# Two silus at a time in the loop, roundings by ScalarE behind it, and the last scales ahead of the comparison

## The chip, the core and the metric

The kernel runs on one core of a Trainium2 chip. The metric is the device time of one execution in microseconds (us). A core has TensorE (PE in the profile: matmuls and transpositions), VectorE (DVE), ScalarE (ACT), GpSimd (POOL), and SyncE (SP), which issues transfers. Each engine takes its own list of instructions in order; semaphores make it wait for the others.

## The reference

One transformer layer on x of 2048 tokens with 256 features, and a context of 1601 tokens of 256 features:

```
# cross attention: latents are the layer-normalised x, keys are context and latents
q = LN(latents) @ W_q;  k, v = concat(LN(ctx) @ W_kv, LN(latents) @ W_kv)
sim  = rms(q) * scale @ rms(k).T           # 4 heads of 64, masked context keys at -max
x    = x + softmax(sim) @ v @ W_out + b_out
# feed-forward on y = layernorm(x), hidden size 1024
aq(t) = clip(round(t * s), -128, 127) / s, s = 127 / max|t| per token
wq(w) = ternary weights over their mean magnitude
h = aq(y) @ wq(w1).T
h = depthwise convolution over tokens, three taps and a bias, for each hidden channel
h = silu(h)
out = x + aq(h) @ wq(w2).T
```

Rounding to integers is done by adding a large constant (MAGIC, 12582912) and taking it off again: in f32 the addition leaves an integer.

## The kernel before

`layer` is written twice: once with a cheap bound for the softmax shift (`behind` is a tile that receives a flag), and a second time, exact, behind a branch that runs only if the flag counts a row for which the bound was too far off. In the runs shown the second copy is not entered. All instructions are issued through a helper (`InOrder`, line 170) that keeps them in the written order on each engine, so nearly all rows of the profile say L170 and are told apart by their tiles.

**Prologue.** Normalised tokens are projected to q, k and v, and the two weights w1 and w2 are made ternary.

**Loop.** There are eight units (four groups of 512 queries, two pairs of heads each) of ten beats; a beat takes three blocks of 128 keys, the last beat of a unit two. In a beat TensorE makes the scores of the next beat (`st<-q_un,kT`), ScalarE takes their exponentials (`pt<-st`), and TensorE multiplies the present beat's exponentials with v (`ot<-pt,v_sb`). `pt` has six buffers; the score banks ("big") have three, and are shared with the feed-forward. The rows of exponentials are summed partly by VectorE (`vec`), partly by adding transfers (`acc`, `acd`) that POOL issues.

The feed-forward is laid beside the attention by a plan: `at(k, call, when)` notes a call for beat k. It works in groups g of 256 tokens (0 to 7), each of four slots (two chunks of 128 hidden channels a slot). A slot's calls in `feed_forward` (982) are `hidden` (matmuls to `ph`), `dequantize` (VectorE, `h`), `taps` and `last_tap` (ScalarE's `side`, VectorE's and POOL's `pre`), and `silu` (858), which writes `t`. A slot follows two beats (`pace`) after the one before it; its silu stands three beats after its taps. `t` is kept as token by channel with four channels side by side, so a silu writes one f32 every 16 bytes. When a group's slots are done, `magnitudes`, `columns` and `scales` find each token's largest value, `scales_spread` brings the scales back to rows (`tb`), `rounding` (945) multiplies `t` by them and writes the integers to `hq`, and `product` and `output` finish (`py`, `res`). The silu and the exponential stand in different tables of ScalarE, so the program holds a table load (ACT_TABLE_LOAD) wherever the one follows the other. Groups 0 to 3 and the first slot of group 4 have their silus inside the loop.

**Tail.** Behind the loop, `tick(i)` (1150) takes the remaining 15 slots one after another, `head(i)` (1119) first finishes the last four blocks of 128 tokens of the attention (`block_steps`: divide, output projection `po`, residual, normalise `y`, `quantize` (760) to `yq`, and a transposition), and what the plan still holds (group 3's spreading, roundings and products) is taken one call a tick. A tick's order is: silu of the slots two and one ticks ago, `dequantize` of this slot (`h`), outputs that are due, last tap of the slot before, this slot's `pre` and `side` on ScalarE, a group's scales or roundings where they are due, then the `hidden` matmuls of the next slot and the convolution of this one. `ph` has two buffers, so the next `hidden` waits until the silu of the slot before has read its own. A group's two roundings stand in two successive ticks, and its two products behind the second.

At the end group 7 is rounded in four quarters, and `flag` (1134) compares the last unit's denominators, reduces the result over all units, and sums it over the partitions by a matmul (`many`), whose count is copied to `behind`. It comes ahead of `scales_spread` of group 7 there.

Of the kernel before, what the change touches and what calls it, by code (L numbers as in the profile page):

```python
# [10 lines left out]
F32 = mybir.dt.float32  # L11
# [8 lines left out]
P = 128  # L20
# [9 lines left out]
def layer(  # L30
# [62 lines left out]
    ones16 = const.tile([P, P], BF16, name="ones16")  # L93
    nc.vector.memset(ones16, 1.0)

    neg_half = const.tile([P, 2 * H], F32, name="neg_half")
    nc.gpsimd.memset(neg_half, -0.5)

# [530 lines left out]
    with att:  # L629
# [86 lines left out]
                        start=(n == 0), stop=(n == len(terms) - 1),  # L716
                    )

        def compare(u, r):

            if behind is None:
                return
            within = wk.tile([P, QW], BF16, tag="within", name="within")
            vector.tensor_scalar(within, r, math.exp(LAG), None, ALU.is_le)
            vector.scalar_tensor_tensor(within, r, math.exp(-LAG), within, ALU.is_ge, ALU.mult)
            vector.tensor_reduce(near[:, u : u + 1], within, AX.X, ALU.min)


        def block_steps(qb, oT, sub, po):
            box = {}  # L730

            def project_out():
                box["po"] = po()
                for c in range(ND):
                    tensor.matmul(
                        box["po"], oT[:, c, ts(sub, P)], wo_sb[:, c, :],
                        start=(c == 0), stop=(c == ND - 1),
                    )

            def residual():  # L740
                vector.tensor_tensor(x1[qb], box["po"], x1[qb], ALU.add)
                st = sm.tile([P, 6], F32, tag="st3", name="st3")
                box["mv"] = sm.tile([P, 2], F32, tag="mv3", name="mv3")
                vector.bn_stats(st, x1[qb])
                vector.bn_aggr(box["mv"], st)

            def inverse_deviation():
                inverse_root(box["mv"][:, 1:2], LN_EPS, ALU.add, P, (1,), gpsimd)

            def normalize():  # L750
                box["y"] = wk.tile([P, D], F32, tag="y", name="y")
                vector.tensor_scalar(
                    box["y"], x1[qb], box["mv"][:, 0:1], box["mv"][:, 1:2], ALU.subtract, ALU.mult
                )
                vector.tensor_reduce(
                    units1[:, qb : qb + 1], box["y"], AX.X, ALU.max, apply_absolute_value=True
                )
                box["sc"] = quant_scales(units1[:, qb : qb + 1], 1, vector)

            def quantize():  # L760
                vector.tensor_scalar(box["y"], box["y"], box["sc"][:, 0:1], None, ALU.mult)
                box["yq"] = wk.tile([P, D], BF16, tag="yq", name="yq", bufs=2)
                vector.tensor_scalar(box["yq"], box["y"], MAGIC, -MAGIC, ALU.add, ALU.add)

            def transpose():

                t0 = OFF + qb * P
                tp = bank("tpy", [P, 2, P])
                yT = tp[:, 0, :].bitcast(BF16).rearrange("p (c t) -> p c t", c=ND)
                for c in range(ND):  # L770
                    tensor.transpose(yT[:, c, :], box["yq"][:, ts(c, P)], ident16)
                tensor.transpose(tp[:, 1, :], box["cm"][:, 0, :], ident)
                scalar.copy(xq_all[:, :, t0 : t0 + P], yT)
                scalar.copy(ib_all[:, 1 + qb * P : 1 + (qb + 1) * P], tp[:, 1, :])

            def bias():
                gpsimd.tensor_tensor(x1[qb], x1[qb], bo_sb, ALU.add)

            def unit_row():
                product_units(units1[:, qb : qb + 1], 0)  # L780
                box["cm"] = as_rows(units1[:, qb : qb + 1], 1)

            return (
                bias, project_out, residual, inverse_deviation, normalize, quantize, unit_row,
                transpose,
            )
# [158 lines left out]
        def rounding(g, i, tokens=slice(0, G)):  # L945
            b = groups_[g]
            t = b["t"][i][:, tokens, :]
            vector.tensor_tensor(
                t, t, b["tb"][:, tokens].unsqueeze(2).to_broadcast(list(t.shape)), ALU.mult
            )  # L950
            if "hq" not in b:
                b["hq"] = fp.tile([P, G, NH], BF16, tag="hq", name="hq", bufs=1)
            vector.tensor_scalar(
                b["hq"][:, tokens, ts(i, NC2)], t, MAGIC, -MAGIC, ALU.add, ALU.add
            )

        def product(g, i):
            b = groups_[g]
            py = b["py", i] = where["py"]()
            for c in range(NH):  # L960
                tensor.matmul(
                    py, b["hq"][:, ts(i, P), c], w2T[:, c, :], start=(c == 0), stop=(c == NH - 1)
                )
# [18 lines left out]
        def feed_forward(g, k, slots, pace=2):  # L982

            for n in range(slots):
                s, t = g * NP + n, k + n * pace
                for m, call in (
                    (-1, hidden), (-1, dequantize), (0, taps), (1, last_tap), (3, silu),
                ):
                    at(t + m, lambda call=call, s=s: call(s), LATE)
                if n % 2:  # L990
                    at(t + 4, lambda n=n: magnitudes(g, n // 2), LATE)
            if slots < NP:
                return
            t = k + NP * pace
            for m, call in (
                (3, columns), (3, scales), (5, scales_spread), (5, lambda g: rounding(g, 0)),
                (6, lambda g: rounding(g, 1)), (7, lambda g: end_product(g, 0)),
                (7, lambda g: end_product(g, 1)),
            ):
                at(t + m, lambda call=call: call(g), LATE)  # L1000
# [130 lines left out]
                if i < NSUB:  # L1131
                    run(i, RESIDUAL, INVERSE)

        def flag():

            compare(len(units) - 1, r)
            if behind is None:
                return
            worst = sm.tile([P, 1], F32, tag="worst", name="worst")
            vector.tensor_reduce(worst, near, AX.X, ALU.min)  # L1140
            vector.tensor_scalar(worst, worst, 0.5, None, ALU.is_lt)
            many = y_bank("many")[:, :1]
            tensor.matmul(many, ones, worst, start=True, stop=True)
            vector.tensor_copy(behind, many)

        rest = [call for key in sorted(plan) for call in plan.pop(key)]
        slots = list(range(4 * NP + 1, NG * NP))
        N = len(slots)

        def tick(i):  # L1150

            at_ = {i - ((g - 4) * NP - 1) + (g == NG - 1): g for g in range(4, NG)}
            if 0 <= i - 2 < N:
                end_silu(slots[i - 2], 1)
            if 0 <= i - 1 < N:
                end_silu(slots[i - 1], 0)
            if i < N:
                dequantize(slots[i])
            if i >= N and 0 <= i - 1 < N:
                end_last_tap(slots[i - 1])  # L1160
            if 6 in at_:
                magnitudes(at_[6], 1)
                columns(at_[6])
            while outputs:
                output(*outputs.pop(0))
            if 0 <= i - 1 < N and i < N:
                end_last_tap(slots[i - 1])
            if i < N:
                end_taps(slots[i])
            if 6 in at_:  # L1170
                scales(at_[6], at_[6] == NG - 1)
                if at_[6] == NG - 1:
                    flag()
            if 7 in at_ and at_[7] != NG - 1:
                scales_spread(at_[7])
                rounding(at_[7], 0)
            if 8 in at_ and at_[8] != NG - 1:
                rounding(at_[8], 1)
            if 4 in at_:
                magnitudes(at_[4], 0)  # L1180
            if 7 in at_ and at_[7] == NG - 1:
                g = at_[7]
                scales_spread(g, True)
                for n in range(QPG):
                    for half in range(2):
                        rounding(g, half, ts(n, P))
                    product(g, n)
                for n in range(QPG):
                    output(g, n)
            if i + 1 < N:  # L1190
                hidden(slots[i + 1])
            if i < N:
                end_convolve(slots[i])
            if 1 <= i <= NSUB:
                run(i - 1, TURN)
            if 8 in at_ and at_[8] != NG - 1:
                for n in range(QPG):
                    end_product(at_[8], n)
# [54 lines left out]
```

## Time and profile before

| | |
|---|---|
| median of 3 runs (lowest, highest) | 685.49 us (684.77, 688.87) |
| the profiled execution | 688.55 us |
| its span, first to last instruction | 686.7 us |
| busy PE, DVE, ACT, POOL | 629.2, 464.1, 423.8, 276.6 us |
| mean granted TensorE clock | 0.972 |
| the loop's last attend matmul ends | 591.7 us |
| the last output (`res`) on VectorE | 681.89 us |

In the page each digit of a slice is the busy share in tenths of one fortieth of the span; PEclk is the clock that the throttle grants TensorE. A group's row gives the tile written and those read, the shape, the count, then busy us and mean ns, and the idle time before with what ended it. Lines of the order in time give start and length in us.

### The profile page before, as it was taken

What the parts mean: (1) busy time and instruction counts of PE and PEld (TensorE: products, weight loads), DVE (VectorE), ACT (ScalarE), POOL (GpSimd) and SP (SyncE); (2) the same over time, 40 slices, a digit from 0 to 9 for tenths busy, and PEclk for the clock granted to TensorE, in tenths of its full rate; (3) what the DMA queues carried; (4) which work ended last, traced back from release to release, by engine and by line L of the source; (5) the groups of instructions that cost most, each with busy time, mean ns of one, the idle gap of its engine ahead of it and who ended that gap; (6) DMA issues with size and microseconds to landing.
All of it is one profiled execution on the core that took longest, in us unless ns stands there. A gap on an engine that the chain in (4) does not pass through costs nothing. (4 is left out here: it accounts for less than half of the span.)

```text
span 686.7 us, 8000 instructions
## 1 busy us (share of the span) xinstructions
PE 629.2 (92%) x2796; PEld 266.3 (39%) x2796; DVE 464.1 (68%) x770; ACT 423.8 (62%) x535; POOL 276.6 (40%) x331
## 2 busy tenths in 40 slices
PE   4999898999999999999999999998899999857754
PEld 2555563333333333333334333332333333345542
DVE  3658774332832766596378779757966797897885
ACT  1656556554556445669945469998765789545540
POOL 2656673221221234244245433425354446742330
PEclk9999999999999999999999999999999999997975
DMA  7600003685878674478849447693564576100001
GB/s 241 170 0 0 1 1 92 128 161 111 167 140 183 128 148 93 93 154 152 185 96 172 101 107 154 125 182 94 107 123 92 132 138 114 31 0 16 16 16 36
DMA packets 32220, 72.12 MB, mean 105 GB/s; under 512 B 7531, under 2 KB 16940, under 8 KB 32172
## 3 DMA queue, kind: packets, MB, share of 16 engines
q0 software_dynamic: 16560, 60.30, 43.3%
q1 hardware_dynamic: 14524, 10.45, 5.1%
q10 hardware_dynamic: 1088, 0.79, 0.4%
q8 instruction: 24, 0.39, 0.2%
q14 instruction: 24, 0.20, 0.1%
HBM read 9.13 MB, written 2.10 MB: 16 GB/s over the span
## 5 line engine op out<-in xcount | busy, mean ns | idle before, releaser
L170 ACT ACTIVATE pt<-st,bias 128x1024 f32<-128x1024 f32 x232 | 242.8, 1112 | 123.1 <-issue 64.6
L170 PE MATMUL st<-q_un,kT 64*128 64x512 f32 x928 | 223.7, 611 | 4.7 <-DVE res L170 1.8
L170 PE MATMUL ot<-pt,v_sb 128*64 128x512 f32 x928 | 216.6, 600 | 0.0
L170 DVE TENSOR_TENSOR vec<-vec,pt 128x1024 f32<-128x1024 f32 x107 | 136.7, 1278 | 40.2 <-ACT pt L170 36.3
L170 PEld LDWEIGHTS st<-q_un,kT 64*128 64x128 f32 x928 | 83.0, 187 | 124.8 <-issue 91.3
L170 PEld LDWEIGHTS ot<-pt,v_sb 128*64 128x64 f32 x928 | 60.2, 136 | 136.7 <-issue 130.4
L170 POOL DMA_DIRECT2D acd<-pt x54 | 44.9, 831 | 127.9 <-ACT pt L170 61.4
L170 POOL DMA_DIRECT2D acc<-pt x61 | 52.7, 865 | 69.4 <-ACT pt L170 51.7
L170 POOL TENSOR_TENSOR pre<-pre,side 128x512 f32<-128x512 f32 (+1 forms) x32 | 38.3, 1196 | 62.3 <-DVE pre L170 51.4
L170 ACT ACT_TABLE_LOAD x34 | 43.6, 1283 | 16.6 <-DMA lb<-in_L_xattn_ln_l_b_dram 7.4
L170 PE MATMUL kv<-wkv_sb,feat 128*128 128x512 f32 (+1 forms) x116 | 52.9, 599 | 0.0
L170 POOL TENSOR_TENSOR ss<-ss,neg_half 128x8 f32<-128x8 f32 (+1 forms) x23 | 39.1, 1702 | 1.9
L170 ACT ACTIVATE t<-pre 128x512 f32<-128x512 f32 (+1 forms) x32 | 29.7, 928 | 11.8 <-POOL pre L170 11.6
L170 POOL TENSOR_SCALAR cm<-ones,units 128x128 f32<-128x128 f32 x16 | 11.8, 739 | 61.4 <-DVE units L170 57.9
L170 DVE COPY oT<-ot 128x512 f32<-128x512 f32 x8 | 5.5, 691 | 44.6 <-PE ot L170 44.6
L170 DVE TENSOR_REDUCE ss<-sq 128x8 f32<-128x512 f32 (+1 forms) x23 | 15.5, 672 | 29.0 <-ACT sq L170 28.9
L170 DVE TENSOR_TENSOR h<-ph,ib_all 128x516 f32<-128x516 f32 x32 | 21.9, 686 | 19.0 <-PE ph L170 18.6
L170 PE MATMUL ph<-h,dg 128*128 128x256 f32 x90 | 25.8, 428 | 7.4 <-DVE h L170 7.4
L170 DVE RECIPROCAL r<-dn 128x512 f32<-128x512 f32 (+1 forms) x11 | 27.3, 2478 | 5.7 <-PE dn L170 5.7
L170 PEld LDWEIGHTS kv<-wkv_sb,feat 128*128 128x128 f32 (+1 forms) x116 | 21.2, 192 | 21.9 <-issue 20.9
L170 ACT ACTIVATE side<-h,cw_sb 128x256 f32<-128x256 f32 x66 | 29.6, 506 | 0.0
L170 PE MATMUL py<-w2T,hq 128*128 128x256 bf16 x128 | 20.8, 317 | 7.2 <-DVE hq L170 7.2
(129 smaller groups left out, 708.9 us busy)
## 6 DMA issues: line engine op xcount, KB each, us to landing
acc<-pt POOLq DMA_DIRECT2D x61, 512.0 KB, 5.1
acd<-pt POOLq DMA_DIRECT2D x54, 512.0 KB, 4.8
tok<-in_x_dram SPq DMA_DIRECT2D x4, 512.0 KB, 6.1
w_sb<-in_L_ffn_w_dram SPq DMA_DIRECT2D x4, 512.0 KB, 5.3
q_un<-in_x_dram SPq DMA_DIRECT2D x4, 512.0 KB, 3.9
out_dram<-res SPq DMA_DIRECT2D x16, 128.0 KB, 1.7
tok<-in_ctx_dram SPq DMA_DIRECT2D x3, 512.0 KB, 4.7
wkv_sb<-in_L_xattn_W_kv_dram ACTq DMA_DIRECT2D x1, 512.0 KB, 7.2
```

The lines of the kernel that those rows point to most:

```text
L170: return tc.keep_in_program_order(getattr(self.engine, name)(*args, **kwargs))
```

## The change

Three edits, besides a small constant tile `magic` that holds MAGIC and -MAGIC for ScalarE's bias.

1. In the loop the silu of an even slot is put off by one `pace`, to the beat of the following odd slot's silu, so that both run one behind the other.
2. Behind the loop the rounding of `yq` (last four blocks) and of `hq` (groups 3 to 6) is done by two ScalarE instructions each in place of one of VectorE; for `yq` the multiplication by the scale goes along with the first of them. The multiplication of `t` by its scales stays on VectorE, and group 7 keeps its old way.
3. At the end only the two comparisons of the flag stay where they were; the reductions and the sum over partitions come after the first half of group 7's roundings, and the copy to `behind` after its products. The transposition of group 7's scales so comes ahead of the sum.

```diff
-        def compare(u, r):
-
-            if behind is None:
-                return
+        def bounds(r):
             within = wk.tile([P, QW], BF16, tag="within", name="within")
             vector.tensor_scalar(within, r, math.exp(LAG), None, ALU.is_le)
             vector.scalar_tensor_tensor(within, r, math.exp(-LAG), within, ALU.is_ge, ALU.mult)
-            vector.tensor_reduce(near[:, u : u + 1], within, AX.X, ALU.min)
+            return within
...
             def quantize():
+                box["yq"] = wk.tile([P, D], BF16, tag="yq", name="yq", bufs=2)
+                if qb >= NQB - NSUB:
+                    scalar.activation(
+                        box["y"], box["y"], AF.Identity, bias=magic[:, 0:1], scale=box["sc"][:, 0:1]
+                    )
+                    scalar.activation(box["yq"], box["y"], AF.Identity, bias=magic[:, 1:2])
+                    return
                 vector.tensor_scalar(box["y"], box["y"], box["sc"][:, 0:1], None, ALU.mult)
-                box["yq"] = wk.tile([P, D], BF16, tag="yq", name="yq", bufs=2)
                 vector.tensor_scalar(box["yq"], box["y"], MAGIC, -MAGIC, ALU.add, ALU.add)
...
-            vector.tensor_scalar(
-                b["hq"][:, tokens, ts(i, NC2)], t, MAGIC, -MAGIC, ALU.add, ALU.add
-            )
+            hq = b["hq"][:, tokens, ts(i, NC2)]
+            if where["later"] and g < NG - 1:
+                scalar.activation(t, t, AF.Identity, bias=magic[:, 0:1])
+                scalar.activation(hq, t, AF.Identity, bias=magic[:, 1:2])
+            else:
+                vector.tensor_scalar(hq, t, MAGIC, -MAGIC, ALU.add, ALU.add)
...
                 s, t = g * NP + n, k + n * pace
+
+                last = 3 if n % 2 or slots == 1 else 3 + pace
                 for m, call in (
-                    (-1, hidden), (-1, dequantize), (0, taps), (1, last_tap), (3, silu),
+                    (-1, hidden), (-1, dequantize), (0, taps), (1, last_tap), (last, silu),
                 ):
...
-        def flag():
-
-            compare(len(units) - 1, r)
-            if behind is None:
-                return
+        def flag(within):
+
+            u = len(units) - 1
+            vector.tensor_reduce(near[:, u : u + 1], within, AX.X, ALU.min)
             worst = sm.tile([P, 1], F32, tag="worst", name="worst")
             vector.tensor_reduce(worst, near, AX.X, ALU.min)
             vector.tensor_scalar(worst, worst, 0.5, None, ALU.is_lt)
             many = y_bank("many")[:, :1]
             tensor.matmul(many, ones, worst, start=True, stop=True)
-            vector.tensor_copy(behind, many)
+            held["many"] = many
...
                 scales(at_[6], at_[6] == NG - 1)
-                if at_[6] == NG - 1:
-                    flag()
+                if at_[6] == NG - 1 and behind is not None:
+                    held["within"] = bounds(r)
...
                     for half in range(2):
                         rounding(g, half, ts(n, P))
+                    if n == 0 and behind is not None:
+                        flag(held["within"])
                     product(g, n)
+                if behind is not None:
+                    vector.tensor_copy(behind, held["many"])
                 for n in range(QPG):
                     output(g, n)
```

In the list of each engine this takes 16 table loads from ScalarE and adds 24 of its instructions; VectorE loses eight `hq`, four `y` and four `yq` instructions and gains two small constant fills at the start; on TensorE only the `many` matmul changes places with group 7's transposition (`tpb`); the lists of POOL and SP are the same as before.

## Prediction

> **What bounds the kernel now.** I read the slices of the page first, then busy time by stretches, the groups kept apart by shape, and the order in time around the places that change.
>
> ```profile
> PE   4999898999999999999999999998899999857754
> DVE  3658774332832766596378779757966797897885
> ACT  1656556554556445669945469998765789545540
> PEclk9999999999999999999999999999999999997975
> ```
>
> Two regimes: up to slice 34 TensorE is at nine tenths; behind it TensorE falls, VectorE leads and the clock drops in places.
>
> ```profile
> 230.00:592.00 362.00, 354.84 (x1599) 129.19 (x1595) 267.76 (x386) 261.13 (x294) 158.65 (x183) 1.00 0.63 129
> 592.00:630.00 38.00, 25.36 (x117) 16.71 (x117) 31.11 (x74) 14.13 (x31) 14.26 (x24) 0.87 0.01 4
> 630.00:660.00 30.00, 21.74 (x128) 16.83 (x127) 27.18 (x46) 18.31 (x35) 10.54 (x13) 0.99 0.07 23
> 660.00:683.00 23.00, 12.65 (x49) 7.83 (x47) 17.05 (x32) 4.40 (x9) 3.35 (x4) 0.57 0.06 20
> ```
>
> Behind the length stand PE, its loads, DVE, ACT and POOL busy, then clock and DMA. From 230 to 592 TensorE works 354.8 of 362.0 us: the loop is TensorE's. In the tail VectorE works 31.1 of 38 and 27.2 of 30 us: the tail hangs on it and on the chains through it.
>
> **The pairing of the silus.** Each silu in the loop costs ScalarE two table loads, silu's and then exp's again.
>
> ```profile
> L170 ACT ACTIVATE pt<-st,bias 128x1024 f32<-128x1024 f32 x232 | 242.8, 1112 | 123.1 <-issue 64.6 <-PE st L170 43.8 <-DMA acc<-pt 7.7
> L170 ACT ACT_TABLE_LOAD x34 | 43.6, 1283 | 16.6 <-DMA lb<-in_L_xattn_ln_l_b_dram 7.4 <-issue 6.2 <-PE st L170 2.1
> L170 ACT ACTIVATE t<-pre 128x512 f32<-128x512 f32 x17 | 19.5, 1150 | 0.2
> ```
>
> Sixteen slots become eight pairs: 16 loads go, 16 x 1.283 = 20.5 us of ScalarE. The Trainium skill ("ScalarE: Activation LUTs", "Table sets: the hidden batching unit") says to batch activations by table set, and "What ACT_TABLE_LOAD costs" prices a switch at 2.66 us with its drain: 42.6 us by the page, 20.5 by the row, and the trace sides with the row: the load at 584.66 below is followed by its silu at 585.96, with no drain between. On the path either is worth almost nothing, by the waits of 230 to 592:
>
> ```profile
> PE st L170 <- ACT pt L170: 0.8, 2, 0.4
> ```
>
> TensorE waited 0.8 us for an exponential there; gain 0 to 0.8, I take 0. A pair's block is 1.28 + 1.15 + 1.1 + 1.28 = 4.8 us against 3.7 for a single one; a beat takes TensorE 5.5 us and ScalarE 3.1 (three exponentials), so it catches up under the cover of six pt buffers and three score banks. The cover ends with the loop.
>
> ```profile
> 581.53 3.11 ACT L170 ACTIVATE pt<-st,bias 128x1024 f32<-128x1024 f32 x3
> 584.66 1.28 ACT L170 ACT_TABLE_LOAD   x1
> 585.96 1.16 ACT L170 ACTIVATE t<-pre 128x512 f32<-128x512 f32 x1
> 587.13 1.28 ACT L170 ACT_TABLE_LOAD   x1
> 588.42 2.12 ACT L170 ACTIVATE pt<-st,bias 128x1024 f32<-128x1024 f32 x2
> ```
>
> The last pair's block stands before the last two exponentials. It starts at 584.66 as before, since what precedes it waited for a DMA's landing (until 578.3), which isn't touched. They end at 591.6, not 590.5. TensorE's last four attend matmuls (0.95 us, ended 591.7) need the second one, and end at 592.6. All of the tail follows: **+1.0 us** (0 to 1.2).
>
> **The roundings.** Eight hq writes of 128x1024 (g3 to g6) and four y, yq pairs leave VectorE. Each hq takes 0.6 to 1.1 us until the next instruction, 6.9 in sum; y and yq 0.68, so 2.7: relief 9.6 us. ScalarE gets two instructions for each hq, +MAGIC in place and then -MAGIC, the second waiting for the first. The row for 128x1024 is the exponential's, 1.11 us: 2.25 for a pair, 18 us for eight. The y pairs cost 0.60 + 0.49 by the tail's 128x256 pre and side, 4.4 us. Together 22 us.
>
> Is 1.11 right for hq, written in runs of 8 bytes with gaps of 8? The silu of 128x512 takes 1.150 us though half as large; it writes single f32 16 bytes apart. "SBUF — State Buffer" (the note on cachelines under "Door 1") says that SBUF has 16-byte lines and wants two hits in each for full rate. Silu has one, hq four: by the rule 1.11, by the silu row's rate about 2.05. The silu row agrees with the rule; no row shows ScalarE writing four of eight. I take 1.11 and keep 2.05 for the range.
>
> Against the edit speaks "ScalarE: Activation LUTs", "Rules for kernel authors": adds and multiplies belong on VectorE. By that rule alone it loses 22 - 9.6 = 12.4 us. The trace decides by who waits, so I replay the group from h at 645.04 to h at 659.61, 14.57 us.
>
> ```profile
> 647.40 1.22 DVE L170 TENSOR_TENSOR t<-t,tb 128x1024 f32<-128x1024 f32 x1 [1.29 <-ACT tb L170]
> 648.66 0.69 DVE L170 TENSOR_SCALAR hq<-t 128x1024 bf16<-128x1024 f32 x1
> 649.27 0.69 DVE L170 TENSOR_TENSOR h<-ph,ib_all 128x516 f32<-128x516 f32 x1
> 651.52 1.11 DVE L170 TENSOR_SCALAR hq<-t 128x1024 bf16<-128x1024 f32 x1
> 655.67 0.70 DVE L170 TENSOR_TENSOR h<-ph,ib_all 128x516 f32<-128x516 f32 x1
> ```
>
> With the first line's start kept, the multiply lasts until 648.6. VectorE goes on to the next h at 648.65, 0.6 early, and to the second multiply, done by 650.9. ScalarE, in order, rounds from 648.7 to 650.95; only then come its two silus (0.47 apart). The one that frees ph runs 651.35 to 652.05, where it ran 648.67 to 649.40 before, so the next hidden matmuls start at 652.1, not 649.44, and their h at 652.7. ScalarE's pre and side of that tick end near 652.7, the second rounding runs until 655.0, and the product's last 12 matmuls (1.53 us) start at 655.1 instead of 652.69 and end at 656.6. Its outputs (res) stand ahead of the last tap and the following h on VectorE: res until 657.1, tap until 657.5, h from 657.5 instead of 655.67. The remainder, 3.94, is unchanged. So the group takes 16.4 us: +1.85. Two groups show it (g4's and g5's roundings): **+3.7**. Behind g6's no h follows, but the last silu stands behind the second rounding, and the last maximum waits for it: multiply from 662.90 to 664.1, rounding until 666.4, two silus until 667.3, rounding until 669.6, silu until 670.2, maximum from 670.3 instead of 668.83: **+1.5**.
>
> Front (h at 599.76 to h at 630.37, g3's pairs and the four y): until the fifth h VectorE gains 2.7 + 1.8 = 4.5 us. Then h needs hidden, hidden the silu of ph, and that silu stands behind two xq, ib copies (0.5), a rounding (2.25), y and yq (1.1) and another silu (0.5), 4.35 us in all, and the copies wait for a convolution and the transposition of yq behind it (1.53 + 0.1); the lead is lost and 6.0 us stand in the way: -4.5 + 6.0 = **+1.5** (-4.5 to +4).
>
> **The last scales.** Before: from qsc at 672.60 the flag's five VectorE steps, the matmul, the copy, and then the multiply at 676.40. After: the transposition waits for ScalarE's cm alone, so the multiply starts at 674.6, 1.8 earlier. But flag comes after two of the four multiply pairs (1.1 us on VectorE), and its matmul precedes the product's in TensorE's list, which starts near 678.3, not 677.61; its 16 matmuls take 3.8 to 4.2 us at this clock, then paced by TensorE alone. -1.2 to +0.5; **+0.2**. SP and POOL keep their lists, so no DMA changes its place; behind is copied later, yet before the last res.
>
> **Sum.** 1.0 + 3.7 + 1.5 + 1.5 + 0.2 = +7.9 us. The profiled execution took 688.55 us (span 686.7, the rest lies around it) and would take 696.4; it lies 3.06 over the median of the runs. From 685.49 that is **693.4 us**.
>
> **Rivals.** *VectorE's relief arrives, faster.* In the replayed group the delay of the silu and of hidden (2.7 us) meets a cover: hidden ended at 650.0 before, while its h ran only at 653.68, 3.6 us. With VectorE 1.6 us faster (0.6 + 1.0) 2.0 remain. If a rounding held hidden up by less than that, the 9.6 would come through: 9.6 - 1.0 = 8.6 less, 677 us. For it: VectorE is at 27.2 of 30. Against: two dependent 1.11 us. *hq at the silu's rate:* 0.94 x 8 = 7.5 more, 700.9 us; for it the silu row, against it the rule on lines. *A draw:* lead and delay cancel in front and groups, only the loop's end shows: 686.5. *The pairing pays:* 0.8 at most, inside the draw.
>
> **Numbers.** ScalarE's in-order delay, 693.4: 60%, its own range 689 to 699; 14 of these 60 lie within 1%. hq slow: 14%. Relief: 11%. Draw: 15%. About 1% (6.9 us) is what a measurement here tells from no change. Slower by more: 46 + 14 = 60%; within: 14 + 15 = 29%; faster: 11%. The range goes to 683 and 703: TensorE is busy less densely, and the throttle, 0.57 behind 660, may bite more; 677 and a slow hq with such a clock stay outside.
>
> **Right or wrong.** Table loads 18. From 230 to 592 no gain. The last ot near 592.6. In the tail ScalarE over 50 us, with TensorE's hidden waiting for ScalarE's t, h to h per group near 16.4. If the groups take under 14 us, the replay is wrong; if the hq rows show 2 us, its size is.

## The result, and the profile after

The changed kernel takes **697.8 us** (median of 6 runs, 697.15 to 699.57) beside 686.2 for the kernel before on the same chip (6 runs, 684.77 to 688.87): ratio 1.0165, 95% interval 1.0151 to 1.018. It is slower, by 11.6 us in the medians, where 693.4 was forecast. The profiled execution took 697.66 us, its span is 695.9 us against 686.7.

The slices of the page, as shown of before: the loop's part is much the same. In the last six slices VectorE's digits were 8 9 7 8 8 5 and are 7 5 6 6 6 5, and the clock is below nine in the last five slices, where it was in three of the last four.

```profile
PE   4999898999999999999999999998999999647653
...
DVE  3658774333732864795487679568777878756665
ACT  2566556555554555568844468777476589376760
...
PEclk9999999999999999999999999999999999977885
```

The same stretches as before (length, then busy PE, its loads, DVE, ACT and POOL, clock, DMA share, GB/s; the last one is longer by what the kernel is):

```profile
230.00:592.00 362.00, 355.29 (x1601) 129.01 (x1599) 268.36 (x388) 239.82 (x277) 158.39 (x183) 1.00 0.63 129
592.00:630.00 38.00, 22.21 (x101) 15.05 (x98) 24.87 (x57) 19.34 (x40) 13.35 (x22) 0.83 0.00 0
630.00:660.00 30.00, 20.33 (x107) 15.82 (x106) 20.52 (x34) 22.22 (x38) 9.41 (x11) 0.90 0.06 18
660.00:692.00 32.00, 17.12 (x85) 12.39 (x83) 20.56 (x41) 13.19 (x23) 5.20 (x6) 0.76 0.08 27
```

In the loop ScalarE lost 21.3 us of work (261.13 to 239.82) and TensorE's 355 us did not move. In the tail VectorE fell from 31.11 to 24.87 and from 27.18 to 20.52 us, ScalarE rose from 14.13 to 19.34 and from 18.31 to 22.22, and the clock from 630 to 660 went from 0.99 to 0.90. The wait that grew is TensorE's for ScalarE. From 592 on, by the waits (total, times, longest), first before, then after:

```profile
PE ph L170 <- ACT t L170: 5.6, 5, 1.7
```

```profile
PE ph L174 <- ACT t L174: 20.2, 6, 4.9
```

Where the 9.2 us between the two spans lie, by the starts of VectorE's `h` (h0 is the tail's first; h6, h10 and h14 are those of the last slots of groups 5, 6 and 7), the last `qsc` and the last `res`:

| stage | before | after | difference | forecast |
|---|---|---|---|---|
| to the loop's end (first `tpa`) | 591.61 | 590.63 | -0.98 | +1.0 |
| to h0 | 8.15 | 8.15 | 0 | 0 |
| front, h0 to h6 | 30.61 | 34.39 | +3.78 | +1.5 |
| two groups, h6 to h14 | 29.24 | 34.65 | +5.41 | +3.7 |
| behind g6, h14 to last scale | 12.99 | 13.05 | +0.06 | +1.5 |
| last scale to last `res` | 9.29 | 8.53 | -0.76 | together +0.2 |
| last `res` to the end | 4.81 | 6.50 | +1.69 | |
| span | 686.7 | 695.9 | +9.2 | +7.9 |

The median moved by more than the spans since the profiled execution of before lay 2.35 us above its own median and that of after 0.13 below. The spans are read to 0.1 us, and the line of the end with them. The loop's end wanders in the runs below from 589.3 to 593.1 whatever the edit, so that line carries little. The front's +3.78 is loose too. Two runs below, edit 3 alone and the early copy, leave the front as it was, and their fronts take 29.89 and 29.88 us at a clock of 0.89 in place of 30.61 at 0.83, with the same work on VectorE and ScalarE (before, then edit 3 alone):

```profile
599.76:630.37 30.61, 19.64 (x91) 14.27 (x92) 26.71 (x66) 13.51 (x31) 10.11 (x18) 0.83 0.02 5
```

```profile
598.68:628.57 29.89, 19.45 (x90) 14.24 (x91) 26.73 (x66) 13.49 (x31) 10.11 (x18) 0.89 0.02 5
```

A front read from one profile is uncertain by these 0.7 us.

### The profile page after: what moved, and what is told of

Its sections match the earlier page's. It is cut to its first block, busy times and chain, and to the rows that moved or that the text cites. A ratio compares the mean times of both kernels' runs of the same rounds, so it can differ in the third digit from the quotient of the medians.

```text
span 695.9 us, 7999 instructions
## 1 busy us (share of the span) xinstructions
PE 629.7 (90%) x2796; PEld 268.1 (39%) x2796; DVE 455.9 (66%) x756; ACT 420.6 (60%) x543; POOL 276.6 (40%) x331
## 5 line engine op out<-in xcount | busy, mean ns | idle before, releaser
L174 PE MATMUL ph<-xq_all,w1T 128*128 128x258 bf16 x128 | 20.2, 282 | 21.1 <-ACT t L174 20.2
L174 ACT ACTIVATE t<-pre 128x512 f32<-128x512 f32 (+1 forms) x32 | 27.9, 923 | 8.0 <-POOL pre L174 7.9
```

The source lines that it names most:

```text
L174: return tc.keep_in_program_order(getattr(self.engine, name)(*args, **kwargs))
```

## The experiments

Kernels with one edit alone stand on the kernel before; the later ones on these or on the changed kernel. A difference in us is the ratio's excess times 687.2, the median of before in the longer comparisons.

### Edit 1 alone: the pairing

```diff
+                last = 3 if n % 2 or slots == 1 else 3 + pace
...
-                    (-1, hidden), (-1, dequantize), (0, taps), (1, last_tap), (3, silu),
+                    (-1, hidden), (-1, dequantize), (0, taps), (1, last_tap), (last, silu),
```

> The kernel before with the paired silus alone. The prediction's step: loop work of TensorE unchanged, last attend matmul 1.0 us later (592.7), time +1.0 us. The reading of the trace after: a reload of exp waits for the scores that its exponential needs, so with TensorE just behind it the 1.28 us are exposed; eight of these go, one of them at a unit's start near 493 us is worth 1.6 to 1.8 us, and 0.8 us come back at the loop's end: last attend matmul near 590.7, time -1.0 us. Rival (the pairing is what made the kernel slower, by longer ScalarE blocks): +3 us or more.

Ratio 1.0008 (0.9998 to 1.0019, 22 runs): +0.5 us, no difference that it can tell; the 1.0 us less that the reading of the changed kernel's trace had promised did not come. The waits from 560 to 600 of this kernel have a line that the kernels without pairing lack:

```profile
PE ot L170 <- ACT pt L170: 0.8, 1, 0.8
```

Sixteen table loads, 20.5 us of ScalarE, are worth nothing in the loop, and TensorE waits 0.8 us for the last pair at its end.

### The roundings of hq alone, and of y alone

```diff
-            vector.tensor_scalar(
-                b["hq"][:, tokens, ts(i, NC2)], t, MAGIC, -MAGIC, ALU.add, ALU.add
-            )
+            hq = b["hq"][:, tokens, ts(i, NC2)]
+            if where["later"] and g < NG - 1:
+                scalar.activation(t, t, AF.Identity, bias=magic[:, 0:1])
+                scalar.activation(hq, t, AF.Identity, bias=magic[:, 1:2])
+            else:
+                vector.tensor_scalar(hq, t, MAGIC, -MAGIC, ALU.add, ALU.add)
```

> The kernel before with only the hq roundings (groups 3 to 6) on ScalarE; silus single, yq and the flag as before. Theory (ScalarE's order delays the silu that frees ph and the product): h to h over the groups near 16.5 to 17.3 us instead of 14.6, time +7 to +10 us. Rival (VectorE's relief covers it, the loss comes from the flag's place and the clock at the end): -1 to +2 us.

Ratio 1.0087 (1.0069 to 1.0106): **+6.0 us**, a little under the 7 expected. The groups take 17.49 and 17.35 us, as in the changed kernel (17.39 and 17.26): their loss is this edit's alone. The front takes 32.17, +1.56. TensorE's wait for the silu from 592 on (5.6 us before):

```profile
PE ph L174 <- ACT t L174: 15.7, 5, 3.9
```

> The kernel before with only y and yq of the last four blocks on ScalarE. Theory: 0.68 us of VectorE against 1.1 us of ScalarE for each of four, in the stage where VectorE is the tighter of the two: -1 to +1 us. Rival (any rounding on ScalarE is a loss there): +3 us, h to h over the first six slots longer than 30.6 us.

With y and yq alone (the diff of `quantize` above) the ratio is 0.9996 (0.9986 to 1.0006), and the front 29.87, 0.74 less than before. That is the length of the fronts that nothing was changed in (29.89 and 29.88, at the same 0.89), so no gain there is shown to be y's.

### Edit 3 alone: the flag behind the transposition

> The kernel before with only the flag's reductions, sum and copy moved behind half of the last roundings. The prediction: +0.2 us. The reading of the trace after: SyncE reads behind ahead of issuing the last two outputs, and now waits for it; the last res comes 0.5 us earlier or at the same time, the span ends 1 to 2 us later behind it: +1 us. Rival (the earlier transposition pays): -1 us or less.

Ratio 1.0016 (1.0006 to 1.0027): +1.1 us. The last `res` came 8.70 us behind the last scale (before 9.29), yet the end 6.26 us behind that `res` (before 4.81).

The four parts sum to 0.5 + 6.0 - 0.3 + 1.1 = 7.3 us; all together gave 11.3. Of the 4.0 between, 3.0 stand in the front, as far as single profiles tell: 0.8 for the two roundings one at a time, 3.78 with both; counted from a front of 29.9 us it is 2.2. The rest is within the intervals.

### Half the delay: one ScalarE instruction for each hq

```diff
-                scalar.activation(t, t, AF.Identity, bias=magic[:, 0:1])
                 scalar.activation(hq, t, AF.Identity, bias=magic[:, 1:2])
```

This kernel leaves out the addition of MAGIC, so hq is not rounded.

> The kernel with only the hq roundings on ScalarE (groups 3 to 6), each with one instruction instead of two: the addition of MAGIC into t is left out, so hq isn't rounded. Theory (ScalarE's order delays hidden and the product; the prediction put the turning point at a delay of 2.0 us, and half a rounding delays by 2.7 - 1.15 = 1.5): VectorE's relief comes through, h to h per group about 14.4 us or less instead of 17.4, time 2 us under the kernel before, 8 us under the one with both instructions. Rival (the loss comes from handing hq to another engine at all, by an added wait and not by its length): groups above 16 us, +4 us.

Ratio 0.9978 (0.9965 to 0.999), 1.5 us **faster** than before; groups 14.52 and 14.49, clock 1.00. In order of time, one group of it:

```profile
645.47 1.15 ACT L174 ACTIVATE hq<-t,magic 128x1024 bf16<-128x1024 f32 x1 [1.29 <-DVE t L174]
...
646.97 0.68 ACT L174 ACTIVATE t<-ph,cb_sb 128x256 f32<-128x256 f32 x1
...
648.61 0.68 DVE L174 TENSOR_TENSOR h<-ph,ib_all 128x516 f32<-128x516 f32 x1
...
649.43 1.91 PE L174 MATMUL py<-w2T,hq 128*128 128x256 bf16 x16
```

The silu that frees `ph` (`t<-ph`) starts 1.50 us behind the rounding's start, and the next h 3.26 us behind the one at 645.35. One dependent instruction of 1.15 us is hidden; two are not. The groups get no shorter than before all the same: hidden waits 2.27 us for the silu (0.82 before), and VectorE's outputs then wait 1.21 us for the product, which stands behind hidden on TensorE.

### The roundings behind the next silus

```diff
+                pending.append((t, hq))
...
+            late_rounding()
...
-            if 8 in at_ and at_[8] != NG - 1:
+            if 9 in at_ and at_[9] != NG - 1:
                 for n in range(QPG):
-                    end_product(at_[8], n)
+                    end_product(at_[9], n)
```

`late_rounding` issues both instructions of each pending hq; it stands behind the next tick's silus, `pre` and `side`.

> The kernel with only the hq roundings on ScalarE, but each issued behind the next tick's silus, pre and side, and the products of groups 4 to 6 one tick later. The same instructions, 18 us of ScalarE. Theory (their place in ScalarE's list is what costs): hidden no longer waits for them, groups near 14.5 to 16 us, time -1 to +2 us against the kernel before. Rival (the ScalarE work itself is too much for the tail): still +5 us or more.

Ratio 1.0033 (1.0022 to 1.0043): +2.3 us. The later place takes 3.7 of the 6.0 us away. The groups fall to 15.94 and 16.01, not to 14.6: the silu is free, but the products and with them the outputs come a tick later (from the last scale to the last `res` it is 12.67 us, 9.29 before), and the clock stays at 0.89. This run doesn't separate the two.

### Only the first hq on ScalarE, behind the next silus, with y and yq there

```diff
+            if where["later"] and g < NG - 1 and i == 0:
+                pending.append((t, hq))
...
+            late_rounding()
```

> The kernel before with y and yq on ScalarE, and of the hq roundings only the first of each group, issued behind the next tick's silus; the second stays on VectorE. Theory (half of the load fits into ScalarE's gaps and nothing that TensorE needs stands behind it): groups near 14.2 us, time -2 to -3 us against the kernel before, the fastest of all. Rival (any rounding on ScalarE costs): +2 us.

Ratio 0.9963 (0.9946 to 0.998, 14 runs, median 684.89): **2.5 us faster than before**, the best version found. Groups 15.07 and 14.53 (expected near 14.2), front 30.17: neither holds the gain. By the profile it lies behind g6, where h14 to the last scale takes 10.75 us and 12.99 before, with a clock of 0.89 and 0.63; how much of that is the clock's is not separated.

### TensorE kept busy in the changed kernel

```diff
+            if i < N and (i in (2, 3) or 7 in at_ or 8 in at_):
+                for n in range(6 if 8 in at_ else 24):
+                    tensor.matmul(
+                        chunk[slots[i]]["ph"][:, 1, G + 2 : G + 254], w1T[:, 0, 0:P],
+                        xq_all[:, 0, 0:252], start=True, stop=True,
+                    )
```

> The changed kernel with added TensorE matmuls whose result is never read (252 columns, 24 or 6 of them) behind the convolutions of the ticks in which TensorE waits for ScalarE's roundings. They fill idle time only. Theory (the roundings' waits also let TensorE's clock fall, which costs 0.9 us in each group on the product and over 2 us in front): clock 1.0 in the groups instead of 0.90, h to h 16.4 instead of 17.3, and the front 2 us shorter; time -3 to -5 us against the changed kernel, that is +6 to +8 against the kernel before. Rival (the clock doesn't matter, ScalarE alone sets the pace): no change against the changed kernel, +11 us.

Ratio 1.0081 (median 692.86 of 6 runs) in place of 1.0165: 5 to 6 us back from matmuls that nobody reads (the filled-up kernel, below). By stretches (front, two groups, behind g6; the clock stands third from the end):

```profile
601.23:632.68 31.45, 21.71 (x135) 17.61 (x136) 23.30 (x56) 21.34 (x43) 10.12 (x18) 0.95 0.01 5
632.68:649.26 16.58, 13.86 (x100) 11.79 (x99) 11.96 (x21) 12.39 (x22) 5.90 (x7) 1.00 0.08 25
649.26:665.73 16.47, 13.29 (x92) 10.72 (x91) 11.29 (x20) 12.40 (x22) 5.20 (x6) 1.00 0.05 16
665.73:678.48 12.75, 7.70 (x53) 5.70 (x51) 7.90 (x13) 8.03 (x12) 3.75 (x4) 1.00 0.01 3
```

With the clock at 1.00 a group takes 16.58 and 16.47 us, so the excess of the changed kernel's groups over the replay is TensorE's clock. The front takes 31.45 at 0.95, where the changed kernel's took 34.39 at 0.80.

### The copy to behind early

```diff
             tensor.matmul(many, ones, worst, start=True, stop=True)
-            held["many"] = many
+            vector.tensor_copy(behind, many)
```

> The kernel before with edit 3 alone, as in the run of edit 3 alone, but the comparison's result is copied to behind directly after the count `many`, ahead of the two last copies of outputs and not behind the new transposition's work. Theory (GpSimd's closing work, a queue counter 0.86 us and a drain 2.80 us, starts only when behind has been read, and edit 3 made it the last thing to end): from the last res to the end of the span 4.8 us again in place of 6.26, from the last scale to the last res at most 0.6 us more than the 8.70 of edit 3 alone; time about 1 us under that run, 687.0 within 0.7. Rival (the later end has another cause, such as SyncE's load of behind ahead of the last outputs' transfers): last res to end stays near 6.3 and the time near 688.

Ratio 1.0000 (0.9989 to 1.0012) against 1.0016 with the late copy; last scale to last `res` 8.71, last `res` to end 4.83, both as expected; the intervals of the two ratios overlap, so the time alone doesn't settle it. Counted from the last scale the copy comes 1.4 us earlier (5.25 us behind it, 6.61 with the late copy). The theory can be read more sharply in the profiles: in all twelve the end of the span is the later of 8.33 us behind the start of the copy to `behind` and 4.81 us behind the start of the last `res`, within 0.1 us (one within 0.2). The copy is the later in three of them, in bold below, and with the early copy the two are level; a program without GpSimd's drain was not tried.

| kernel | copy + 8.33 | last res + 4.81 | end |
|---|---|---|---|
| before | 684.2 | **686.7** | 686.7 |
| after | **695.9** | 694.2 | 695.9 |
| edit 3 alone | **685.3** | 683.8 | 685.3 |
| early copy | **684.8** | **684.8** | 684.8 |
| filled up | **693.4** | 692.0 | 693.4 |

### The best version with TensorE kept busy

```diff
+                if at_[6] == NG - 1:
+                    keep_warm(24, where["ph"]("warm"))
...
+                keep_warm(6, where["ph"]("warm"))
...
+            if i in (1, 2, 3, 4, N - 1):
+                keep_warm(24 if i == N - 1 else 12, chunk[slots[i]]["ph"])
```

`keep_warm(n, ph)` issues n matmuls like those of the kernel above.

> The run with y on ScalarE and the first hq of each group there behind the next silus (684.89), with matmuls added whose result nobody reads: 12 in the front's four ticks, 24 in the last tick, 24 and 6 behind the last group's two transpositions. If TensorE's clock costs there as the filled-up changed kernel showed (front 2 to 3 us, end about 1 us): granted clock near 1.00 in the front and behind the last group, and 1 to 3 us less, 682 to 684. Rival (the front and the end are set by VectorE's and ScalarE's chain of products and roundings, and the added matmuls stand ahead of needed ones): clock up, time the same or more, 685 to 687.

Ratio 0.9973 (0.9964 to 0.9983, median 685.47), beside 0.9963 without the added matmuls: no gain, the rival's forecast. The mean clock rose from 0.980 to 0.987, but in the profiled execution the front took 32.16 us (30.17 without) and h14 to the last scale 13.29 (10.75). That execution lies 4.7 us above the median of its runs, so these two sizes are not typical; that a higher clock buys nothing here is shown by the times, why it doesn't is not settled.

## Why the prediction was right, and where it was off

The mechanism was the likeliest case's: ScalarE, in order, holds the silu back that frees `ph`, and hidden, h and the outputs follow. Its size was less good: +11.6 us in the medians where +7.9 was forecast. That the two profiles differ by 9.2 is luck in part: front, groups and end lie 4.7 us over their forecasts, the loop's end and the stage behind g6 3.4 under. So is the nearness of the 12.4 us that the sum of busy times gave: the same `hq` instructions at a later place in ScalarE's list cost 2.3 us, not 6.0. Point by point:

**Loop, right.** Table loads are 18, the loop gained nothing, and TensorE waits at its end as worked out:

```profile
584.00 2.13 ACT L174 ACTIVATE t<-pre 128x512 f32<-128x512 f32 x2
...
586.15 1.28 ACT L174 ACT_TABLE_LOAD   x1
...
587.45 2.12 ACT L174 ACTIVATE pt<-st,bias 128x1024 f32<-128x1024 f32 x2
...
588.61 2.08 PE L174 MATMUL ot<-pt,v_sb 128*64 128x512 f32 x8 [0.81 <-ACT pt L174]
...
590.63 0.44 PE L174 MATMUL tpa<-ident,m 128*128 128x128 f32 x2
```

Both silus (584.00), the load, the last two exponentials until 589.57, and the last attend matmuls behind 0.81 us of waiting. Forecast +1.0, shown 0.8 and timed +0.5 (-0.1 to +1.3). Where the loop ended in this profile was luck of the execution: 590.6, not 592.6.

**Size of the rounding, right.** 1.11 us for a run of 128x1024 was taken, 2.05 kept as the rival:

```profile
L174 ACT ACTIVATE hq<-t,magic 128x1024 bf16<-128x1024 f32 x8 | 9.2, 1149 | 0.3
L174 ACT ACTIVATE t<-t,magic 128x1024 f32<-128x1024 f32 x8 | 9.1, 1142 | 4.1 <-DVE t L174 4.1
```

**The groups: steps right, one term missing.** One group of the changed kernel (h at 650.56), to be laid beside the replay:

```profile
654.11 1.15 ACT L174 ACTIVATE t<-t,magic 128x1024 f32<-128x1024 f32 x1 [1.29 <-DVE t L174]
...
655.29 1.15 ACT L174 ACTIVATE hq<-t,magic 128x1024 bf16<-128x1024 f32 x1
...
656.79 0.66 ACT L174 ACTIVATE t<-ph,cb_sb 128x256 f32<-128x256 f32 x1
...
657.51 0.60 PE L174 MATMUL ph<-xq_all,w1T 128*128 128x258 bf16 x4 [3.36 <-ACT t L174]
...
657.95 2.46 PE L174 MATMUL ph<-h,dg 128*128 128x256 f32 x6
...
658.15 0.69 DVE L174 TENSOR_TENSOR h<-ph,ib_all 128x516 f32<-128x516 f32 x1 [0.81 <-PE ph L174]
659.28 1.15 ACT L174 ACTIVATE hq<-t,magic 128x1024 bf16<-128x1024 f32 x1
...
660.20 2.63 PE L174 MATMUL py<-w2T,hq 128*128 128x256 bf16 x16
...
663.88 0.70 DVE L174 TENSOR_TENSOR h<-ph,ib_all 128x516 f32<-128x516 f32 x1
```

Counted from h, the rounding was forecast at 3.7 and stands at 3.55, the silu at 6.3 (6.23), hidden at 7.1 (6.95), its h at 7.7 (7.59), the second rounding's end at 10.0 (9.87). VectorE waits, as foretold, for hidden, and hidden 3.36 us for ScalarE's t. Then the times part: six convolution matmuls take 2.46 us, not 1.46 as in the filled-up kernel, and the product is done at 12.3, not at 11.6; the remainder from that h (663.88) to the next group is 3.94, exactly the one taken over. By stretches of this group:

```profile
650.56:657.50 6.94, 2.87 (x15) 1.81 (x14) 5.56 (x8) 5.41 (x10) 3.74 (x4) 1.00 0.00 0
654.84:658.25 3.41, 0.74 (x6) 0.68 (x6) 2.60 (x4) 3.38 (x7) 1.58 (x1) 1.00 0.00 0
658.25:661.67 3.42, 3.42 (x13) 2.51 (x12) 0.59 (x1) 3.39 (x5) 0.00 (x0) 0.50 0.00 0
661.67:667.80 6.13, 4.48 (x32) 3.75 (x30) 5.01 (x11) 2.78 (x7) 1.45 (x2) 1.00 0.13 43
```

The granted clock is halved right behind the wait of 3.36 us, from 658.25 to 661.67, just when TensorE has everything to do, and is 1.00 before and after. The Trainium skill ("TensorE: Matmul & The Clock Gate", "Part 1: The HAM clock gate") says that an idle window of about 3.4 us halves the clock and as long a busy one restores it. The rows agree in the main: the halved stretch is 3.42 us long and TensorE is busy in all of it. But the 3.41 us ahead of it were not idle throughout; TensorE was busy in 0.74 of them. The prediction took the convolution's and product's durations from a group at 0.98; it named the throttle as a reason for a wide range, but gave the wait that it added no such term in the sum. That missing term is 17.3 - 16.4, **0.9 us a group**: +3.7 became +5.4, and with the clock held at 1.00 it is 16.5.

**Behind g6: delay right, its cover missed.** From the multiply to the last maximum 7.4 us were forecast, and 7.32 measured (670.19 to 677.51; before 5.93): +1.4. But the multiply starts 2.37 us behind h14, not 3.29, in a stage whose clock was better (0.79, 0.63 before), and the way from the maximum to the scale takes 3.36, not 3.77: 0.9 and 0.4 back. +1.5 became +0.06 by that; that the clock is the cause of the 0.9 and 0.4 is not shown. Pairs of kernels at like clock give +0.1 (12.96 for the pairing alone, 13.04 for hq alone, both at 0.76) and +1.0 (12.07 for y alone at 0.80, 13.05 here at 0.79), so its size stays open between these.

**Front: mis-sized by both terms.** Up to the fifth h VectorE gained 3.1 us, not 4.5: `q_un` waited 0.96 us for `po` (0.17 before) and one `y` took 0.82 us in place of 0.40. Then the order came as told:

```profile
617.19 2.76 PE L174 MATMUL ph<-h,dg 128*128 128x256 f32 x6
...
620.41 0.38 ACT L174 COPY xq_all<-tpy 128x256 bf16<-128x256 bf16 x1 [3.34 <-PE tpy L174]
...
620.84 1.16 ACT L174 ACTIVATE t<-t,magic 128x1024 f32<-128x1024 f32 x1
...
623.09 0.58 ACT L174 ACTIVATE y<-y,magic,qsc 128x256 f32<-128x256 f32 x1
...
624.56 0.66 ACT L174 ACTIVATE t<-ph,cb_sb 128x256 f32<-128x256 f32 x1
...
625.27 1.02 PE L174 MATMUL ph<-xq_all,w1T 128*128 128x258 bf16 x4 [4.89 <-ACT t L174]
...
626.38 0.69 DVE L174 TENSOR_TENSOR h<-ph,ib_all 128x516 f32<-128x516 f32 x1 [6.97 <-PE ph L174]
```

From the copy of xq to the silu of ph ScalarE needs 4.15 us (forecast 4.35), but the copy itself waited 3.34 for the transposition behind a convolution of 2.76 us, where 1.53 was put in. The h at 626.38 stands 8.05 us behind the one before it, against 1.21: 6.8 in the way, not 6.0. With the last 0.02 up to h6 that is -3.08 + 6.84 + 0.02 = +3.78. Filled up, at a clock of 0.95, the front takes 31.45: 0.8 over that of before, which itself ran at 0.83, and 1.6 over the unchanged fronts at 0.89. So 2.9 of the 3.8 us come back when TensorE is kept busy, and the chain through ScalarE costs 1.6 or more at a like clock.

**The last scales: the wrong step was to put the later copy at nothing.** "Copied later, yet before the last res" came true (687.54 and 689.40), and the stage itself won 0.8 us, within its bounds. But all five engines read `behind` ahead of their closing work, and GpSimd's consists of a branch, a queue's counter and a drain, in the changed kernel (duration min/median/max in ns, first and last start in us)

```profile
L1239 POOLq TENSOR_LOAD <-behind x1: 492/492/492, 687.7 to 687.7; - x1
```

```profile
L1240 POOLq COMPARE_BRANCH  x1: 45/45/45, 688.3 to 688.3; - x1
...
L1240 POOLq INC_SWDGE_SEM  x1: 862/862/862, 691.3 to 691.3; - x1
```

```profile
L1270 POOLq DRAIN  x3: 34/107/2801, 692.2 to 695.6; - x3
L1270 SPq DRAIN  x3: 7/7/12, 693.8 to 695.3; - x3
...
L1270 DVEq DRAIN  x2: 10/14/17, 693.7 to 695.3; - x2
```

and before

```profile
L1248 POOLq DRAIN  x3: 34/107/2801, 680.7 to 686.5; - x3
```

Before, the drain of 2.80 us ran from 680.7, beside the last outputs; now it starts at 692.2, behind the last `res` (689.40), ends at 695.0, 1.1 us after those of SyncE and VectorE (693.8 and 693.7, 0.02 us at most), and sets the end: +1.7 that the sum had at nothing. That "SP and POOL keep their lists" held; what they wait for in them came later.

**Rivals.** VectorE's relief arrives: with one instruction for each hq the delay is 1.5 us, under the turning point of 2.0 that it named, and the time falls; with two it is 2.6 and the time rises, so a turning point lies between these. But it falls by 1.5 us and not by 8.6: the groups stay at 14.5 us, waiting for the product, and the front (29.18) is only 0.7 us under the unchanged ones at a like clock. A slow hq was excluded by its row. The draw and the paying pairing were excluded by the roundings' 6.0 us and the loop's zero.

## What to carry to other kernels

Work moved to a less busy engine is priced by who stands behind it in that engine's order: two dependent instructions of 1.15 us ahead of a silu cost 2.7 us a group (0.9 of it by the clock), one cost nothing, and half of the roundings, placed behind the silus, gained 2.5 us together with y's. When a change adds a wait of a few us on TensorE, price the matmuls behind it at the lower clock too; and before a stage of two profiles is compared, compare its clock. And an instruction that every engine's closing work waits for belongs early, even when its result is off the path.

## What the runs showed of the hardware

In all twelve traces TensorE's granted clock is either 1.00 or 0.50 and changes only at whole steps of 3.413 us, counted from a moment that differs in each execution. Take these steps as windows, and from TensorE's rows the share of each window in which it was busy. At full clock, every window with a share under 0.41 was followed by a halved one, and none with 0.58 or more was; between these both occurred. A halved clock was full again behind each window with a share of 0.79 or more (46 of them) and stayed halved behind each with 0.76 or less (37). In the two traces with three halved windows in an unchanged front it takes 30.61 us, in the two with two of them 29.89 and 29.88.

The closing work of GpSimd takes 8.33 us from the start of the copy of the branch's flag to the end of the span in the three profiles where it is the last to end; elsewhere the end stands 4.81 us behind the start of the last output, within 0.2 us. Matmuls that nobody reads gave 5 us back in one kernel and nothing in another. The loop's end differed between profiled executions by 3.8 us, part of it a wait of TensorE for an output, 1.8 us near 494, that comes and goes with no edit near it. The three latest ends (591.6, 591.9 and 593.1) are those of the executions that had, beside this wait, one window of halved clock behind it, from 495; that the clock is the cause is not shown.
